# A four-layer graph attention kernel on one core: the first weighted row of a tile written into the accumulator bank by VectorE, and three instead of two dense tiles in the last layer

## The chip, the core and the metric

The kernel runs on one core of one Trainium2 chip. The metric is device time in microseconds (us) for one execution of the whole program; lower is better. Engine names: PE is TensorE (PEld its weight loads), DVE is VectorE, ACT is ScalarE, POOL is GpSimd, SP is SyncE. An "own time" is the time of the one execution that was profiled.

## What is computed

3327 nodes with 512 features pass four graph attention layers over one sparse symmetric adjacency matrix (about 16 neighbours in a row, each node its own neighbour). Each layer normalises, cuts at zero, projects, and mixes the neighbours' rows with softmax weights, one set of weights for each head:

```
h = relu(layernorm(x));  v = h @ W              # 8, 4, 1, 8 heads of 64, 128, 512, 64 columns
e[i,j] = leaky_relu(src[i] + dst[j]) where adj[i,j], else -inf
x = x + (elu of) softmax_j(e) @ v               # elu in layers 1 and 2
```

## The kernel before

**Setup.** Nodes are padded to 3328 and stand in 26 tiles of 128. The first 270 us read the adjacency matrix, list each node's neighbours, and sort the nodes by their number of neighbours. `CAPS[t]` is the longest list in sorted tile t: 36, 25, 23, 22, 21, ... down to 11, 467 in all.

**A listed tile** (`Tile`) of a layer is worked in steps of `GROUP` = 4 neighbour slots. For each slot `fetch` (gather at L834, own row by SP at L865) brings 128 rows of 528 floats from the layer's table in HBM, 2112 bytes each; slot 0 in layers 1 to 3 is the tile's own rows, a plain DMA by SP. `scored` forms z on VectorE (L887, L889) and the weights by an Exp on ScalarE (L890). `group` then multiplies each row by its weights on VectorE into the buffer `m` (L916), and TensorE adds the products up in a PSUM bank, `self.po`, by multiplying each of them with the identity (L921). A tile of K slots thus takes K VectorE products of 128x512 and K matmuls of 128x512. When the last slot is in, `divisors` (L926 to L928), `means` (L938) and `added` (L952 to L960) divide the sum and add it to `x`; in layers 0 to 2 the tile is then centred, turned (L450), cut (L457), projected (L468) and its new table row written by SP (L992). A following layer's gathers cannot start before all rows of its table are written. In the last layer `scatter` (L842) writes the tile's output rows by a POOL DMA. Layer 2 has one head; its sum is made on VectorE alone (L909, L911).

**A dense tile** is one of the tiles of highest degree that is not gathered. `DENSE = [0, 1, 9, 2]` says how many a layer has. In layers 1 and 3 the class `Several` works them: for each of 26 source tiles and each half of the heads (52 units u), SP loads half a row of the table and the mask, ScalarE forms the raw weights of 4 heads for n tiles into `r` (`weights`, L1264, 4 ACTIVATEs of 128 x 128n) and scales the features into `vs` (`features`, L1275, L1276), VectorE applies the mask (`masked`, L1280, one instruction of 128 x 512n), and TensorE multiplies (`products`, L1298, 4n matmuls with 130 columns in layer 3). `begin` (L1238, L1240) makes the targets' terms before the first unit, 2n rounds of four small matmuls and an Exp. Before a bank of such sums is used it is filled by a matmul with zeros (L1290). Layer 2's nine dense tiles have a class of their own (`Wholes`, L1150).

**Order.** POOL, PE, DVE and ACT run a written-out order. For each step s of a layer's list: gathers up to `LOOK` = 7 steps ahead, then pieces that were put down for "first" (units' masks and products, transposes), `scored` of step s+1, pieces for "scored" (the next unit's weights and features), `group` of step s, pieces for "last" (divisors, means, projections). The 52 units are spread evenly over the steps but the last 8. Gather buffers `g` are 7 deep, `m` 3 deep. Tiles go from the last (11 slots) to the first. Layer 3 has 24 listed tiles with 111 steps.

**PSUM in a layer with several heads:** pool `o` has 2 banks for the sums, `p` 1 or 2, `t` 1 or 2 (not in layer 3), `w` 1 (layer 1) or 2 (layer 3), `r` one bank for each dense tile, single-buffered.

Of the kernel before, what the change touches and what calls it, by code (L numbers as in the profile page):

```python
# [10 lines left out]
F32 = mybir.dt.float32  # L11
# [7 lines left out]
P = 128  # L19
# [6 lines left out]
BANK = 512  # L26
# [7 lines left out]
FAR = -30000.0  # L34
ROW = 528
GROUP = 4
DENSE = [0, 1, 9, 2]
ND = max(DENSE)
ROUND = 1.5 * 2.0 ** 23

# [454 lines left out]
class Slots:  # L495
# [5 lines left out]
    class Part:  # L501
        def __init__(self, pool, name, blocks):
            self.blocks, c = [], 0
            for t0, t1 in blocks:
                k = CAPS[t0] if t0 >= min(DENSE) else 1
                self.blocks.append((t0, t1, k, c))
# [17 lines left out]
def tile_gat_stack(ctx: ExitStack, tc: tile.TileContext, x, adj, adjT, ws, avs, out):  # L524
# [266 lines left out]
    with cond.Else():  # L791
        tile_gat_lists(tc, x, adj, ws, avs, out, ident, half, slots, L, low, spare, tabx, tabs)
# [3 lines left out]
def tile_gat_lists(ctx: ExitStack, tc: tile.TileContext, x, adj, ws, avs, out, ident, half, slots, L, low, spare, tabx, tabs):  # L796
# [7 lines left out]
    nc = tc.nc  # L804
# [23 lines left out]
    one, zero = [spool.tile([P, 1], F32, name=n, bufs=1) for n in ("one", "zero")]  # L828
# [10 lines left out]
    def scatter():  # L839
        while waiting:  # L840
            dst, t, rows = waiting.pop(0)
            nc.gpsimd.indirect_dma_start(out=dst, out_offset=bass.IndirectOffsetOnAxis(ap=slots(t, 0), axis=0),  # L842
                                         in_=rows, in_offset=None)

    class Tile:
# [51 lines left out]
        def group(self, i):  # L897


            H, K, wt = HEADS[self.l], CAPS[self.t], self.wt  # L900
            D = F // H
            k0, n, g = self.groups[i]
            if H == 1:
                for q in range(n):
                    v = g[:, q, :].rearrange("p (s m) -> p s m", s=2)[:, :, :F // 2]
                    acc = self.po.rearrange("p (s m) -> p s m", s=2)
                    w = wt[:, k0 + q, 0:1]
                    if k0 + q == 0:
                        nc.vector.tensor_scalar(acc, v, w, None, OP.mult)  # L909
                    else:  # L910
                        nc.vector.scalar_tensor_tensor(acc, v, w, acc, OP.mult, OP.add)  # L911
                return
            m = pools["m"].tile([P, GROUP, F], F32, name="m")
            for q in range(n):
                v = g[:, q, :].rearrange("p (s m) -> p s m", s=2)[:, :, :F // 2]
                nc.vector.tensor_tensor(m[:, q, :].rearrange("p (s h d) -> p s h d", s=2, d=D),  # L916
                                        v.rearrange("p s (h d) -> p s h d", d=D),
                                        wt[:, k0 + q, :H].rearrange("p (s h) -> p s h", s=2)
                                        .unsqueeze(3).to_broadcast([P, 2, H // 2, D]), OP.mult)
            for q in range(n):  # L920
                nc.tensor.matmul(self.po, ident, m[:, q, :], start=(k0 + q == 0), stop=(k0 + q == K - 1))  # L921

        def divisors(self):
            H, K = HEADS[self.l], CAPS[self.t]
# [424 lines left out]
    for l in range(NL):  # L1349
        W, following = following, None  # L1350
        if l == NL - 1:
            before.close()
        with ExitStack() as c2:
            def pool(name, bufs, **kw):
                return c2.enter_context(tc.tile_pool(name=f"{name}{l}", bufs=bufs, **kw))

            psum = dict(space=bass.MemoryType.PSUM)
            whole = HEADS[l] == 1
            pools = {"o": pool("ps_o", 1 if whole else 2, **psum)}
            if l < NL - 1:  # L1360
                pools.update(t=pool("ps_t", 1, **psum))
            if whole:
                pools.update(w=pool("ps_w", 3, **psum), e=pool("epool", 1))
                wholes = Wholes(l, W)
                pw = L[:, :BANK]
            else:
                pools.update(m=pool("mpool", 3))
                pools.update(p=pool("ps_p", 1 if DENSE[l] else 2, **psum))
                if DENSE[l]:
                    pools.update(w=pool("ps_w", l // 3 + 1, **psum), r=pool("ps_r", 1, **psum))  # L1370
                    if DENSE[l] > 1:
                        pools.update(e=pool("epool", 1))
                    wholes = Several(l, DENSE[l], W)
                    pw = pools["p"].tile([P, BANK], F32, name="pw")
            if DENSE[l]:

                scores = itertools.cycle([pw[:, :BANK // 2], pw[:, BANK // 2:]])
            else:
                scores = itertools.cycle([pools["p"].tile([P, BANK], F32, name="pw") for _ in range(2)])
            tiles = [Tile(l, t, W) for t in order if t >= DENSE[l]]  # L1380
            steps = [(tl, i) for tl in tiles for i in range(len(tl.k0))]
            if l == 0:
                for t in range(ND):
                    steps.insert(18 + 10 * t, (Mask(t), 0))
                steps[-8:] = [s for i, step in enumerate(steps[-8:]) for s in (step, (Ranked(i), 0))]
                steps += [(Ranked(j), 0) for j in range(8, NT)]
            if whole:
                wholes.place(len(steps) - 8)
            elif DENSE[l]:
                wholes.place(0, len(steps) - 8)  # L1390
            at_end = len(steps) + 12
            fetched = 0
            for s in range(-1, at_end):
                def do(place):
                    for piece in at.pop((s, place), []):
                        piece()
                while fetched < min(len(steps), s + LOOK):
                    steps[fetched][0].fetch()
                    fetched += 1
                do("first")  # L1400
                if s + 1 < len(steps):
                    steps[s + 1][0].scored(steps[s + 1][1])
                do("scored")
                if 0 <= s < len(steps):
                    tl, i = steps[s]
                    tl.group(i)
                    if i == len(tl.k0) - 1:
                        tl.finish(s)
                do("last")
                if s == 16 and l + 2 < NL:  # L1410
                    following = Weights(nc, wpool, work, l + 2, ws, avs)
                if l == 0 and s in (0, 1, 2):
                    for _ in range(3):
                        W.fold()
                if s >= 24 and s % 4 == 0 and following is not None:
                    following.fold()
            scatter()
            assert not at
# [42 lines left out]
```

## Time and profile before

| | |
|---|---|
| Median of 3 runs | 3030.45 us (3009.33 to 3045.77) |
| Profiled execution, own time | 2458.72 us |
| its span, first to last instruction | 2456.9 us |
| PE, DVE, POOL, ACT busy | 2082.3, 1918.9, 1751.1, 911.0 us |
| mean granted TensorE clock | 0.946 |
| gathers begin: layer 0, 1, 2, 3 | 270.9, 923.5, 1480.0, 1930.4 us |
| last gather of the last layer | 2435.1 us |

The stages follow from the gathers' own timeline: a layer's first gather waits for the last row of its table, so the pauses on POOL before 923.5, 1480.0 and 1930.4 us are the borders of the layers. Busy times are sums over an engine's instructions; a busy TensorE is not one at its peak, because matmuls overlap and their ends are modelled.

### The profile page before, as it was taken

To read this page: it belongs to the slowest core of one execution; us is meant where nothing else is said; L and a number is where in the kernel's file an instruction comes from. 1 tells how busy PE (TensorE), PEld (TensorE's weight loads), DVE (VectorE), ACT (ScalarE), POOL (GpSimd) and SP (SyncE) were. 2 spreads that over 40 slices of the span, in tenths; PEclk is the share of its full clock that TensorE was granted. 3 is DMA by queue.
4 is the path that set the end of the run, shared out by engine and by line. 5 is a ranking of instruction groups with operands and counts; after the bars stand their busy time and mean duration, and the time that the engine had idled before them with its cause. 6 is when DMAs were issued, how large, how long until landed. Compare 5 with 4: busy or idle time off the path is not lost. (4 is left out here: it accounts for less than half of the span.)

```text
span 2456.9 us, 26822 instructions
## 1 busy us (share of the span) xinstructions
PE 2082.3 (85%) x6832; PEld 1164.1 (47%) x6832; DVE 1918.9 (78%) x5004; ACT 911.0 (37%) x2506; POOL 1751.1 (71%) x1739
## 2 busy tenths in 40 slices
PE   3788689999998857989999986879696699999897
PEld 1666345455444423545455543445354455455443
DVE  6988787887767736888888865988989488787776
ACT  5877024343331113433333323443333343333330
POOL 7898467777777767776777747676666477777775
PEclk9988899999999988999999997989897899999999
DMA  6886579999988788887888857878776588888885
GB/s 229 320 297 235 173 232 290 291 291 295 278 270 237 229 230 246 263 242 235 247 260 256 253 152 254 252 243 248 217 250 186 165 250 251 242 249 248 242 242 171
DMA packets 262490, 599.55 MB, mean 244 GB/s; under 512 B 103923, under 2 KB 121331, under 8 KB 257974
## 3 DMA queue, kind: packets, MB, share of 16 engines
q0 software_dynamic: 126128, 438.08, 59.5%
q1 hardware_dynamic: 132454, 152.86, 19.3%
q10 hardware_dynamic: 3744, 6.82, 0.8%
q8 instruction: 55, 0.90, 0.1%
q14 instruction: 109, 0.89, 0.1%
HBM read 547.96 MB, written 49.65 MB: 243 GB/s over the span
## 5 line engine op out<-in xcount | busy, mean ns | idle before, releaser
L921 PE MATMUL bank<-m,ident 128*128 128x512 f32 x2608 | 1200.8, 606 | 136.3 <-DVE m L916 135.6
L916 DVE TENSOR_TENSOR m<-g,pw 128x512 f32<-128x512 f32 x1304 | 810.8, 681 | 136.9 <-ACT pw L890 130.3
L834 POOL DMA_INDIRECT g<-tab,idxb x734 | 699.7, 953 | 249.0 <-issue 166.9
L921 PEld LDWEIGHTS bank<-m,ident 128*128 128x128 f32 x2608 | 480.9, 192 | 716.3 <-issue 342.5
L468 PE MATMUL pv<-w,hT 128*128 128x264 f32 x1664 | 436.3, 417 | 66.4 <-ACT hT L457 41.3
L890 ACT ACTIVATE pw<-z 128x32 f32<-128x32 f32 (+4 forms) x362 | 69.8, 193 | 948.8 <-DVE z L889 948.7
L468 PEld LDWEIGHTS pv<-w,hT 128*128 128x128 f32 x1664 | 335.2, 205 | 168.2 <-ACT hT L457 47.5
L834 POOL DMA_INDIRECT g<-tabx,twiceb x342 | 324.2, 948 | 104.8 <-issue 77.1
L834 POOL DMA_INDIRECT g<-tab,idxa x297 | 283.3, 954 | 144.5 <-issue 79.9
L1150 PE MATMUL whole<-ve,em 128*128 128x512 f32 x468 | 230.1, 644 | 45.0 <-DVE em L1123 38.5
L694 POOL TENSOR_TENSOR key<-a,keys 128x3328 int32<-128x3328 int32 (+1 forms) x29 | 189.4, 6536 | 15.9 <-DVE cand L703 11.8
L911 DVE SCALAR_TENSOR_TENSOR bank<-g,L,bank 128x512 f32<-128x512 f32 x243 | 183.2, 754 | 6.8
L887 DVE TENSOR_TENSOR z<-g,pw 128x32 f32<-128x32 f32 (+4 forms) x362 | 63.5, 175 | 149.9 <-DMA g<-tab,idxb 48.2
L1150 PEld LDWEIGHTS whole<-ve,em 128*128 128x128 f32 x468 | 94.0, 206 | 158.2 <-issue 97.1
L834 POOL DMA_INDIRECT g<-tabx,twicea x99 | 94.6, 955 | 69.3 <-issue 32.2
L703 DVE MAX8 cand<-key 128x8 f32<-128x208 int32 x416 | 143.7, 364 | 0.1
L450 PE MATMUL pt<-ident,xn 128*128 128x128 f32 x416 | 67.6, 288 | 50.2 <-ACT hT L457 18.6
L1116 ACT ACTIVATE r<-low,mc,b 128x384 f32<-128x384 f32 x78 | 52.6, 675 | 151.3 <-DVE em L1123 127.8
L1264 ACT ACTIVATE r<-low,spare 128x256 f32<-128x256 f32 x208 | 98.9, 476 | 5.1
L889 DVE SCALAR_TENSOR_TENSOR z<-z 128x32 f32<-128x32 f32 (+5 forms) x434 | 86.1, 198 | 15.1 <-DVE z L887 0.2
L450 PEld LDWEIGHTS pt<-ident,xn 128*128 128x128 f32 x416 | 53.8, 149 | 87.7 <-issue 36.4
L431 POOL TENSOR_TENSOR rstd<-ve,half 128x1 f32<-128x1 f32 x52 | 31.9, 614 | 79.7 <-DVE ve L974 42.5
(180 smaller groups left out, 2161.9 us busy)
## 6 DMA issues: line engine op xcount, KB each, us to landing
a<-in_adj SPq DMA_DIRECT2D x25, 1664.0 KB, 8.5
tab<-v SPq DMA_DIRECT2D x78, 264.0 KB, 3.9
ve<-tab SPq DMA_DIRECT2D x78, 264.0 KB, 3.9
g<-tab SPq DMA_DIRECT2D x66, 264.0 KB, 4.2
tabx<-vx SPq DMA_DIRECT2D x26, 528.0 KB, 5.0
g<-tab,idxb POOLq DMA_INDIRECT x734, 3.9
low<-tab SPq DMA_DIRECT2D x52, 132.0 KB, 3.5
room<-tab SPq DMA_DIRECT2D x52, 132.0 KB, 3.7
```

The lines of the kernel that those rows point to most:

```text
L450: nc.tensor.transpose(pt[:, k, :], xn[:, k * P:(k + 1) * P], ident)
L468: nc.tensor.matmul(pv[:, s, :HF + 8], hT[:, k, :], W.w[:, k, s, :], start=(k == 0), stop=(k == KC - 1))
L694: nc.gpsimd.tensor_tensor(key[:, c:c + quarter], a[:, c:c + quarter], keys[:, c:c + quarter], OP.mult)
L703: nc.vector.max(cand[:, g * 8:(g + 1) * 8], key[:, g * SEG:(g + 1) * SEG])
L834: nc.gpsimd.indirect_dma_start(out=out_, out_offset=None, in_=table, in_offset=bass.IndirectOffsetOnAxis(ap=which, axis=0))
L889: nc.vector.scalar_tensor_tensor(z, z, SLOPE, z, OP.mult, OP.max)
L890: nc.scalar.activation(self.wt[:, k0:k0 + n, :H], z, AF.Exp)
L911: nc.vector.scalar_tensor_tensor(acc, v, w, acc, OP.mult, OP.add)
L916: nc.vector.tensor_tensor(m[:, q, :].rearrange("p (s h d) -> p s h d", s=2, d=D), v.rearrange("p s (h d) -> p s h d", d=D), wt[:, k0 + q, ...
L921: nc.tensor.matmul(self.po, ident, m[:, q, :], start=(k0 + q == 0), stop=(k0 + q == K - 1))
L1150: nc.tensor.matmul(tl.po.rearrange("p (s m) -> p s m", s=2), e[:, q * P:(q + 1) * P], v.rearrange("p (s m) -> p s m", s=2)[:, :, :F // 2], ...
L1264: nc.scalar.activation(self.r[:, h, :], self.a[:, g, :], AF.Relu, bias=-1.0, scale=self.b[:, j, g:g + 1])
```

## The change

Three things are altered. In layers with several heads, the product of slot 0 is written by VectorE to the tile's PSUM bank instead of `m`, and the identity matmul of slot 0 is left out; the remaining matmuls of the tile add to what stands in the bank (`start=False`). At the start of each of these layers both banks of pool `o` are written once by a matmul with zeros. And the last layer has three dense tiles instead of two: tile 2, with 23 slots, is no longer gathered, and `r` takes three banks.

```diff
-DENSE = [0, 1, 9, 2]
+DENSE = [0, 1, 9, 3]
...
             for q in range(n):
                 v = g[:, q, :].rearrange("p (s m) -> p s m", s=2)[:, :, :F // 2]
-                nc.vector.tensor_tensor(m[:, q, :].rearrange("p (s h d) -> p s h d", s=2, d=D),
+
+                out_ = self.po if k0 + q == 0 else m[:, q, :]
+                nc.vector.tensor_tensor(out_.rearrange("p (s h d) -> p s h d", s=2, d=D),
                                         v.rearrange("p s (h d) -> p s h d", d=D),
                                         wt[:, k0 + q, :H].rearrange("p (s h) -> p s h", s=2)
                                         .unsqueeze(3).to_broadcast([P, 2, H // 2, D]), OP.mult)
-            for q in range(n):
-                nc.tensor.matmul(self.po, ident, m[:, q, :], start=(k0 + q == 0), stop=(k0 + q == K - 1))
+            for q in range(k0 == 0, n):
+                nc.tensor.matmul(self.po, ident, m[:, q, :], start=False, stop=(k0 + q == K - 1),
+                                 skip_group_check=True)
...
+            if not whole:
+
+                for _ in range(2):
+                    nc.tensor.matmul(pools["o"].tile([P, BANK], F32, name="bank"), ident,
+                                     zero.to_broadcast([P, BANK]), start=True, stop=True)
```

## The prediction

> **What bounds the kernel now.** I began with the page: span, busy times, costliest groups.
>
> ```profile
> PE 2082.3 (85%) x6832; PEld 1164.1 (47%) x6832; DVE 1918.9 (78%) x5004; ACT 911.0 (37%) x2506; POOL 1751.1 (71%) x1739
> L921 PE MATMUL bank<-m,ident 128*128 128x512 f32 x2608 | 1200.8, 606 | 136.3 <-DVE m L916 135.6
> L916 DVE TENSOR_TENSOR m<-g,pw 128x512 f32<-128x512 f32 x1304 | 810.8, 681 | 136.9 <-ACT pw L890 130.3
> ```
>
> By the sums TensorE looks like the bound, and identity matmuls are over half of it. But the shares average four layers, so next came the busy times in stretches (columns: PE, PEld, DVE, ACT, POOL busy with counts, clock, DMA share, GB/s), one stretch from each of layers 0, 1 and 3.
>
> ```profile
> 297.00:840.00 543.00, 493.38 (x1553) 254.76 (x1554) 421.89 (x1120) 168.03 (x436) 402.60 (x425) 0.98 0.87 268
> 1040.00:1400.00 360.00, 347.05 (x1094) 189.65 (x1093) 309.40 (x822) 137.94 (x423) 261.60 (x276) 1.00 0.84 248
> 1950.00:2436.00 486.00, 448.58 (x1622) 241.32 (x1620) 384.42 (x803) 169.44 (x599) 368.05 (x388) 0.99 0.82 244
> ```
>
> POOL shows only 74 to 76%, the lowest of the three. Its timeline explains that:
>
> ```profile
> 2251.83 0.95 POOL L834 DMA_INDIRECT g<-tab,idxb  x1 [0.30 <-issue]
> 2253.08 0.95 POOL L834 DMA_INDIRECT g<-tab,idxb  x1 [0.30 <-issue]
> 2254.34 0.95 POOL L834 DMA_INDIRECT g<-tab,idxb  x1 [0.30 <-issue]
> ```
>
> Each gather starts 1.25 us after the one before and waits for nothing but "issue". This pitch holds almost without a break from 331 to 910 us and from 1930.4 us to the end: POOL is full there, at a displayed 76%. Layer 3 has 382 gathers and 26 output DMAs on POOL: 382 x 1.2525 + 26 x 1.29 = 512 us, against the 511 from its first gather (1930.4) to where its stream breaks (2441.2). Its waits and its part of the chain agree (us in total, times, longest; then shares):
>
> ```profile
> PE bank L921 <- DVE m L916: 48.7, 39, 10.4
> DVE z L887 <- DMA g<-tab,idxb: 47.5, 41, 2.4
> DVE m L916 <- ACT pw L890: 36.5, 103, 2.8
> POOL g L834 <- DVE m L916: 12.5, 41, 0.3
> ```
>
> VectorE waits for gathers to land, TensorE waits for VectorE, and POOL's wait for a buffer is never over the usual 0.3 us gap. In layer 1 the stream breaks between 1072 and 1222 us, some 16 us beyond the pitch in all. There VectorE is the late one: TensorE waited 12.5 us for L916 and VectorE nothing for L921. So in this execution layers 0 and 3 are bound by POOL, layer 1 by VectorE and POOL; nowhere between the borders does TensorE set the pace.
>
> **What the skill says.** The Trainium skill, "Perfetto Trace Analysis", section "DMA Instruction — SWDGE (GPSIMD)": the profiled end of such a DMA is the end of descriptor generation, not of the data's movement. The trace agrees: 0.95 us on POOL, 3.9 us to landing. "PSUM — Partial Sum Buffer", section "The four PSUM rules": VectorE writes neither set nor clear the written bits, and a matmul without the first flag adds where the bit is set. That is why each bank needs one matmul over its full width before VectorE seeds it, so the change can do what it says; no run here shows this yet. "VectorE: DVE Perf Modes", section "The TRN2 errata": an fp32 tensor_tensor takes (N+151)/0.96 ns, 691 for 512; the trace has 681. It has no price for a PSUM destination; the trace does.
>
> **The change part by part.** Unit prices, from the timelines of layer 3:
>
> ```profile
> 1964.29 1.95 PE L1298 MATMUL whole<-spare,low 128*128 128x130 f32 x16
> 1966.08 7.03 PE L921 MATMUL bank<-m,ident 128*128 128x512 f32 x16
> 1967.23 2.48 DVE L916 TENSOR_TENSOR m<-g,pw 128x512 f32<-128x512 f32 x4 [0.33 <-ACT pw L890]
> ```
>
> An fp32 matmul is two instructions. L921 starts 1.79 us after L1298: eight products, 0.224 us each. The row after L921 starts at 1972.94: eight identity matmuls in 6.86, 0.858 each. Four products on VectorE take 2.48, one alone 0.68, so each further one is 0.60.
>
> 1. Slot 0 to the bank. It takes 26, 25 and 23 identity matmuls from layers 0, 1 and 3: 22.3, 21.5 and 19.7 us of TensorE. The VectorE instruction stays and changes its destination. Instructions that write `bank` take 691 to 694 ns (L938, L952), the tensor_scalar of L909 746; so 74 instructions cost 1 to 5 us of VectorE, none below nothing, since the element count is the same. I take 0: outside 1072 to 1222 us its waits for gathers cover it. No new wait stands in VectorE's order: the bank's last reader is `added` two tiles earlier, before this write on VectorE itself. In layers 0 and 3 the removed matmuls lie beside a full POOL: 0. In layer 1 they help only where TensorE is late, at the end:
>
> ```profile
> 1463.42 1.02 PE L921 MATMUL bank<-m,ident 128*128 128x512 f32 x2
> 1464.48 0.70 DVE L938 TENSOR_TENSOR bank<-bank,den 128x512 f32<-128x512 f32 x1 [6.92 <-PE bank L921]
> ```
>
> VectorE waits 6.92 us, and TensorE had run without a pause since 1428.6, in which only tile 1's slot 0 lies. One matmul: -0.9 us. At layer 0's end TensorE waits for VectorE: 0.
>
> 2. Six zero matmuls, 5.2 us of TensorE at three starts. TensorE there waits 10 us for the first product in layers 1 and 3: 0.
>
> 3. The third dense tile, all in layer 3.
> POOL: tile 2 has 23 slots, one by SP, so 22 gathers go: 22 x 1.2525 = -27.6 us; the 26 output DMAs stay. SP loses one own-row DMA; its 52 mask loads grow from 32 to 48 KB.
> TensorE: 23 identity matmuls more go (-19.7, with part 1 -39.5); 52 units get 4 products more, 208 x 0.224 = +46.6. Net +7.1.
> VectorE: the mask grows from 1024 columns (1.21 us) to 1536; with 256 at 0.413 the slope is 1.04 ns, so 1.74: 52 x 0.53 = +27.7. Gone are 23 products (13.8), six steps' z, their wait for Exp (about 4.3) and a tile's divisors and mean (1.4); net about +9 with the longer dense means.
> ScalarE: 208 ACTIVATEs grow from 476 ns to 585 (slope from 128 columns, 367) or 675 (L1116, 384 columns): +23 to +42, on an engine busy 169 of 486 us: hidden.
> Start: `begin` gets two more rounds of 1.85 us; with the zeros its last Exp would end near 1939.4 instead of 1933.6, 1 us past the first Exp of z (1938.33) queued behind it. Seven buffers cover it: 0, at worst 1.
>
> What is late next? Up to 2410 us, where the units end, TensorE needs 413 of 467 us before. After, 420 of 439: 19 us left, 4%. VectorE's 47.5 us of waiting for gathers lose 27.6 and 9: 11 left. Both still fit, but narrowly: masks come in lumps of 1.74 us, `m` is three deep, `r` single. I charge 5 us, between 0 and 20.
>
> Sum: -27.6 + 5 - 0.9 = -23.5, so the profiled execution goes from 2458.7 to 2435.2, a ratio of 0.9904. The median of the runs is 1.2325 times the profiled execution; nothing in the trace says by what. I carry the ratio over: 3030.45 x 0.9904 = 3001. Were the extra 572 us fixed, it would be 3007; were it all a slower gather, 22 x 1.54 = 34 us, 2996.
>
> **Rivals.**
> B, TensorE sets the pace in the timed runs (a lower clock would stretch them). For it: 85% busy, 96% in layer 1. Against: its waits for L916. Then -22.3 - 21.5 + 7.1 = -36.7, times 1.2325: 2985; with layer 3 still bound by POOL, 2947.
> C, layer 3's gain is swallowed: VectorE or TensorE takes over where POOL lets go. For it: the 11 and 19 us above. Against: gather buffers seven deep. Only the 0.9 remains: 3029.
> D, slower: TensorE's waits for VectorE stay in layer 3 and each unit's longer mask lengthens one. TensorE needs 441 there and waits 48.7, together 490, hidden under POOL's 511. After: 449 + 48.7 + 27.7 = 525, 14 to 16 over 511: with 16, 2475 us, carried over 3050. It decides once waits exceed 483 - 449 = 34 us. Against: with POOL ahead, VectorE finds its gathers landed and its own waits shrink.
> That the bank is not seeded (bits clear) would alter values, not time.
>
> **How the numbers follow.** Forecast 0.48, B 0.12, C 0.20, D 0.20. About 1% is what a measurement of this kernel can tell from no change. The forecast's own range is 2985 to 3015, so nearly half of it is faster by over 1%; with B that makes 0.36. C, the rest of the forecast and a third of D are within 1%: 0.47. D with a longer wait: 0.17. The range reaches from B's lower end to past D: 2950 to 3060.
>
> **What would show it.** Right: 1009 gathers of g by index instead of 1031 (734 + 297) outside layer 0; layer 3's stream near 483 us at the 1.25 pitch; L921 with 2414 instructions; L1298 with 1456; layers 0 and 1 as long as before within 2 us. Wrong: gathers in layer 3 that wait for L916 for over 0.3 us; VectorE waiting for L921 or L1298; ScalarE's features waiting for L1298; layers 0 or 1 shorter by over 5 us.

## The result, and the profile after

The kernel after takes 2979.34 us (median of 4 runs, 2973.41 to 2982.78), the kernel before on the same chip 3019.89 us. The ratio is 0.9854, with a 95% interval of 0.9819 to 0.9889: faster, by about 1.5%. The forecast ratio was 0.9904, on 3030.45 us 3001, a gain of 29 us; 40.6 were measured.

Chips differ here: one execution of either kernel takes about 3000 us on the chip of this result and about 2460 us on the chips of most experiments, so a ratio is always between runs on one chip, and times are read from traces only where both stand near 2460 us. The profiled execution of before shown above, 2458.72 us beside runs of 3030, evidently came from a chip of the second kind.

The page of the kernel after (3000 us chip), the rows that answer to those shown of before:

```profile
PE 2211.9 (74%) x7082; PEld 1246.1 (42%) x7082; DVE 1923.1 (65%) x4968; ACT 934.6 (31%) x2502; POOL 1731.4 (58%) x1717
L923 PE MATMUL bank<-m,ident 128*128 128x512 f32 x2414 | 1232.2, 659 | 335.9 <-DVE m L918 197.3
L918 DVE TENSOR_TENSOR m<-g,pw 128x512 f32<-128x512 f32 x1207 | 752.5, 682 | 384.1 <-ACT pw L890 209.2
L918 DVE TENSOR_TENSOR bank<-g,pw 128x512 f32<-128x512 f32 x74 | 51.5, 696 | 100.7 <-ACT pw L890 69.2
```

From this page counts and unit prices can be read. The identity matmul has 2414 instructions, as predicted. The product is split: 1207 go to `m`, 74 to the bank. A write to the bank costs 14 ns more, 1 us over all 74. Lines have moved by up to three: L916 is now L918, L921 is L923, L1264 is L1267, L1280 is L1283, L1298 is L1301.

One thing more has to be read on this chip, because the forecast was about it: layer 3 of the kernel after does not look as predicted here. The longest of POOL's waits for another engine between 2400 and 2900 us (us in total, times, longest), and the chain of the layer by line (shares of the stretch from 2313 us on):

```profile
POOL g L834 <- DVE m L918: 91.7, 21, 8.2
```

```profile
by line: PE bank L923 28.3%; issue 25.5%; PE whole L1301 13.2%; another core or an unknown queue 9.7%; DVE m L918 8.8%; ACT r L1267 3.7%; ACT L L1278 2.3%; DVE room L1283 2.0%; ACT pw L890 0.8%; DVE z L889 0.7%; DVE z L887 0.7%; POOL g L834
```

POOL waits for VectorE's products, up to 8.2 us at a time, and has a share of under 1% of the chain; TensorE has over 40%. So what follows shows the cause on the chips near 2460 us; that it is the cause of the measured gain on this chip is not shown.

For the times, both kernels were run on one chip near 2460 us (`e1_before` and `e4_both` below). The busy times in stretches (columns: stretch and length, then PE, PEld, DVE, ACT and POOL busy with counts, clock, DMA share, GB/s), first the kernel before, then the kernel after. The stretches are layer 0, layer 1, and layer 3 up to its last gather:

```profile
297.00:840.00 543.00, 489.50 (x1543) 253.65 (x1544) 418.99 (x1114) 168.49 (x436) 401.62 (x425) 0.98 0.87 268
1040.00:1400.00 360.00, 348.25 (x1086) 189.88 (x1086) 309.39 (x823) 136.73 (x418) 261.23 (x277) 0.99 0.84 249
1952.00:2438.00 486.00, 447.97 (x1623) 240.81 (x1621) 385.02 (x805) 169.57 (x599) 368.09 (x388) 0.99 0.83 245
```

```profile
297.00:840.00 543.00, 479.95 (x1498) 247.50 (x1498) 417.36 (x1113) 168.25 (x436) 401.92 (x425) 0.97 0.87 268
1040.00:1400.00 360.00, 338.59 (x1063) 184.97 (x1061) 311.35 (x830) 137.23 (x422) 261.23 (x277) 0.99 0.84 249
1952.00:2409.00 457.00, 447.06 (x1947) 272.44 (x1946) 393.77 (x769) 189.31 (x599) 345.81 (x366) 0.99 0.83 247
```

In layers 0 and 1 TensorE loses about 10 us in each stretch, but POOL issues the same 425 and 277 DMAs in the same time: nothing is won there. In layer 3 the kernel after gets from 1952 to its last gather 29 us sooner, with 22 POOL DMAs fewer.

The layers, each from its first gather to the next layer's, the last to the end of the span (times from POOL's timeline), and layer 3 in its two parts, from the first gather to the last and from there to the end:

| us | layer 0 | layer 1 | layer 2 | layer 3 | its gathers | behind them |
|---|---|---|---|---|---|---|
| before (`e1_before`) | 653.4 | 555.9 | 450.1 | 525.6 | 504.1 | 21.5 |
| after (`e4_both`) | 652.0 | 554.4 | 450.7 | 496.0 | 475.3 | 20.7 |

In neither of the two streams of gathers in layer 3 does POOL idle for more than 0.32 us at once. Layer 3 gives 29.6 of the 30.2 us by which the span is shorter (2458.5 to 2428.3). The waits in layer 3's stretch, first before, then after (engine, who waits for whom: us in total, times, longest):

```profile
DVE z L887 <- DMA g<-tab,idxb: 45.7, 41, 3.2
DVE m L916 <- ACT pw L890: 38.4, 103, 2.9
PE bank L921 <- DVE m L916: 37.4, 38, 2.4
```

```profile
DVE m L918 <- ACT pw L890: 39.1, 77, 4.0
DVE bank L918 <- ACT pw L890: 11.9, 22, 1.9
PE bank L923 <- DVE m L918: 9.8, 10, 3.2
ACT L L1278 <- PE whole L1301: 6.7, 5, 3.3
```

VectorE no longer waits for gathers in this stretch: the 45.7 us are gone from the list. TensorE waits 9.8 us for VectorE instead of 37.4. So POOL is still full, but the others stand close behind it, and the layer has hardly any slack left on any of the three: of 457 us TensorE is busy 447; VectorE is busy 394 and waits 51 for Exp, 445 together; POOL's 366 DMAs at a gap of 0.30 us take 346 + 110 = 456.

### The profile page after: what moved, and what is told of

Its sections match the earlier page's. It is cut to its first block, busy times and chain, and to the rows that moved or that the text cites. A ratio compares the mean times of both kernels' runs of the same rounds, so it can differ in the third digit from the quotient of the medians.

```text
span 2971.7 us, 27155 instructions
## 1 busy us (share of the span) xinstructions
PE 2211.9 (74%) x7082; PEld 1246.1 (42%) x7082; DVE 1923.1 (65%) x4968; ACT 934.6 (31%) x2502; POOL 1731.4 (58%) x1717
## 4 chain that ended last, share of the span: by engine, by line
PE 24%; DVE 18%; issue 14%; another core or an unknown queue 8%; ACT 5%; POOL 3%; DMA 2%; SPq 0%; DVEq 0%; POOLq 0%; ACTq 0%
PE bank L923 16%; DVE m L918 6%; PE pv L468 4%; PE whole L1301 3%; DVE bank L911 3%; POOL g L834 3%; ACT r L1267 1%; DVE z L889 1%; DVE z L887 1%; DVE x L961 1%; PE whole L1153 1%; DMA g<-tab,idxb 1%; DVE em L1126 1%; DVE q L438 1%
## 5 line engine op out<-in xcount | busy, mean ns | idle before, releaser
L923 PE MATMUL bank<-m,ident 128*128 128x512 f32 x2414 | 1232.2, 659 | 335.9 <-DVE m L918 197.3
L918 DVE TENSOR_TENSOR m<-g,pw 128x512 f32<-128x512 f32 x1207 | 752.5, 682 | 384.1 <-ACT pw L890 209.2
L834 POOL DMA_INDIRECT g<-tab,idxb x712 | 678.8, 953 | 482.0 <-issue 197.1
L923 PEld LDWEIGHTS bank<-m,ident 128*128 128x128 f32 x2414 | 488.8, 211 | 942.1 <-issue 582.4
L1301 PE MATMUL whole<-L,room 128*128 128x130 f32 x1248 | 173.3, 290 | 59.9 <-issue 59.5
L1301 PEld LDWEIGHTS whole<-L,room 128*128 128x128 f32 x1248 | 164.7, 202 | 91.4 <-issue 89.7
L475 ACT ACTIVATE v<-pv,rstd 128x528 f32<-128x528 f32 x78 | 54.2, 694 | 274.4 <-remote 126.5
L1267 ACT ACTIVATE r<-low,L 128x384 f32<-128x384 f32 x208 | 121.2, 583 | 16.9 <-remote 9.5
L918 DVE TENSOR_TENSOR bank<-g,pw 128x512 f32<-128x512 f32 x74 | 51.5, 696 | 100.7 <-ACT pw L890 69.2
```

Of the source, the lines that this page charges most:

```text
L834: nc.gpsimd.indirect_dma_start(out=out_, out_offset=None, in_=table, in_offset=bass.IndirectOffsetOnAxis(ap=which, axis=0))
L918: nc.vector.tensor_tensor(out_.rearrange("p (s h d) -> p s h d", s=2, d=D), v.rearrange("p s (h d) -> p s h d", d=D), wt[:, k0 + q, :H].re ...
L923: nc.tensor.matmul(self.po, ident, m[:, q, :], start=False, stop=(k0 + q == K - 1), skip_group_check=True)
L1267: nc.scalar.activation(self.r[:, h, :], self.a[:, g, :], AF.Relu, bias=-1.0, scale=self.b[:, j, g:g + 1])
L1301: nc.tensor.matmul(dst, e[:, h, q * P:(q + 1) * P], mov, start=False, stop=(j == NT - 1), skip_group_check=True)
```

## The experiments

All but two ran on two chips near 2460 us. "Layer 3" is measured as in the table, in one trace of each kernel. Kernels whose layer 3 is the same agree in it within 1 us: 525.6 and 526.5 for the kernel before, 495.9 to 496.0 for three that have both parts there.

**The two parts apart.** The kernel before again; the seeding alone; the third dense tile alone; both.

```diff
 e2_seed_only: the kernel after with
-DENSE = [0, 1, 9, 3]
+DENSE = [0, 1, 9, 2]
 e3_dense_only: the kernel before with
-DENSE = [0, 1, 9, 2]
+DENSE = [0, 1, 9, 3]
```

> The kernel before, unchanged, to have its trace beside the change's (2971.7 us of span, of which layers 0, 1, 2 and 3 take 843, 737, 459 and 658 us by the first gathers at 273.7, 1117.3, 1854.6 and 2313.6 us). The trace seen ahead of the prediction had 653, 557, 450 and 527. Theory T (gathers, as predicted): the new trace of before is as long as the runs, near 3020, layers 0 to 2 equal the change's within 10 us, and layer 3 alone is longer, by about 35 us. Rival S (slot 0): layers 0 and 1 are longer than the change's by 20 us or more in sum, layer 3 about the same.

> Slot 0 written to the bank and the zero matmuls, but two dense tiles in the last layer as before. Theory T (the gain is the shorter stream of gathers in layer 3): same as before, ratio 0.997 to 1.003. Rival S (the gain is the 74 matmuls taken from TensorE, which sets the pace in the timed runs): ratio about 0.985. Half and half: 0.992.

> Three dense tiles in the last layer, slot 0 by TensorE as before. Theory T: ratio 0.987 to 0.99, the whole gain, all of it in layer 3. Rival S: the 23 identity matmuls of tile 2 (19.7 us) go and 208 products (46.6 us) come, so TensorE has 27 us more in layer 3: ratio 1.005 or more. Half and half: 0.993.

> The change itself once more, on the chip of the two halves: ratio 0.982 to 0.989. If the halves add, it is the product of the ratios of the two kernels with one half each; if the third dense tile only pays once slot 0 has made room on TensorE, the product is nearer to 1 than this.

| kernel | median us | ratio to before (95%) | layer 3 |
|---|---|---|---|
| `e1_before` | 2460.1 | 0.9999 (0.999 to 1.0008) | 525.6 |
| `e2_seed_only` | 2461.24 | 1.0007 (0.9998 to 1.0017) | 526.1 |
| `e3_dense_only` | 2432.94 | 0.9886 (0.987 to 0.9903) | 500.7 |
| `e4_both` | 2430.07 | 0.9869 (0.9853 to 0.9886) | 496.0 |

The first was expected near 3020 us, to be laid beside the trace of the result; it ran on a chip near 2460 us, so that comparison could not be made. The seeding alone takes 75 identity matmuls (layer 3 has 24 listed tiles then), 64 us by the 0.858 us of the prediction, off TensorE and is worth nothing. The dense tile alone brings nearly all. Layer 3's stretch of the dense tile alone, its waits (us in total, times, longest), and its chain by line (shares of the stretch):

```profile
1951.00:2408.00 457.00, 454.80 (x1981) 277.63 (x1980) 387.36 (x758) 187.24 (x593) 346.03 (x365) 1.00 0.84 247
```

```profile
DVE m L916 <- ACT pw L890: 56.7, 95, 3.7
ACT L L1275 <- PE whole L1298: 13.4, 6, 3.8
PE bank L921 <- DVE m L916: 2.1, 2, 1.4
```

```profile
by line: PE bank L921 46.4%; PE whole L1298 21.4%; DMA g<-tab,idxa 5.7%; issue 5.1%; DVE m L916 5.0%; POOL g L834 4.4%; ACT r L1264 2.4%; DVE room L1280 2.3%; ACT L L1275 1.6%; DMA g<-tab,idxb 1.5%; DMA out<-x,idxa 0.8%; PE whole L1290 0.8%
```

Without the seeding TensorE is full: 454.8 of 457 us, and two thirds of the chain. The waits suggest that its lateness reaches VectorE by way of ScalarE: the features wait 13.4 us for products (L1298) to be done with their buffers, the Exp behind them in ScalarE's order comes late, and VectorE waits 56.7 us for Exp instead of 38.4 (with both parts 6.7 and 51.0). No gather waits for it: from the first gather to the last there are 475.3 us here too, as with both parts. The lateness comes out behind the last gather, where 25.4 us pass to the end instead of 20.7. With the seeding the chain of the same stretch is shared again, as this line of `e4_both` shows, against that of the kernel before below it:

```profile
by line: PE bank L923 23.4%; DVE m L918 12.2%; PE whole L1301 11.0%; DMA g<-tab,idxb 10.6%; issue 10.1%; ACT r L1267 6.9%; POOL g L834 6.4%; DVE room L1283 4.6%; ACT L L1278 2.8%; DMA g<-tab,idxa 2.4%; ACT pw L890 1.5%; DVE z L889 1.4%; DVE
```

```profile
by line: DMA g<-tab,idxb 28.8%; POOL g L834 18.8%; issue 16.4%; DVE m L916 14.9%; PE bank L921 2.6%; DMA g<-tab,idxa 2.4%; ACT r L1264 1.8%; DVE z L889 1.7%; ACT pw L890 1.6%; DVE low L1280 1.6%; DVE z L887 1.5%; ACT spare L1275 1.2%; DMA o
```

The chain goes from gathers and POOL (the kernel before) to TensorE (dense tile alone) to a mixture (both). In layer 3 the seeding is then worth 4.7 us, all of it behind the last gather, and in the medians 2.9; the two ratios' intervals overlap, so its size is known only to a few us. The product of the two halves' ratios is 0.9893, against 0.9869 with both: the parts help each other a little, by no more than the intervals are wide.

**Seeding in the last layer only.** The kernel after, with slot 0 going to `m` and its matmul kept in layers 0 and 1 (there with `start` again, and without the zero matmuls; these two edits are not shown).

```diff
-                out_ = self.po if k0 + q == 0 else m[:, q, :]
+                out_ = self.po if self.l == NL - 1 and k0 + q == 0 else m[:, q, :]
...
-            for q in range(k0 == 0, n):
+            for q in range(k0 == 0 and self.l == NL - 1, n):
```

> The change with slot 0 written to the bank in the last layer alone; layers 0 and 1 as before. If the 3 us by which the whole change beats the kernel with the third dense tile alone come from layer 3, where TensorE was full: ratio 0.986 to 0.988, like the whole change. If they come from layers 0 and 1: 0.988 to 0.990, like the third dense tile alone.

Measured: 2428.97 us, 0.9865 (0.9845 to 0.9886), layer 3 495.9 us. The whole gain is there: the seeding in layers 0 and 1 adds nothing that can be measured.

**POOL relieved without the dense tile.** In layer 3 the last slot of each listed tile is read by a plain SP DMA of 128 rows instead of a gather: 24 gathers fewer in the kernel before, 23 in the kernel after. The rows are the tile's own, as many bytes as before but not the neighbours', so these kernels do not compute the layer's output; they are for the time alone.

```diff
+                elif l == NL - 1 and k0 + q == CAPS[t] - 1:
+                    nc.sync.dma_start(g[:, q, :], tabs[l % 2][t * P:(t + 1) * P, :])
                 elif l > 0:
```

> The kernel before, but in the last layer the last slot of each of the 24 listed tiles is brought by a plain DMA of SP (the tile's own rows, same bytes) instead of a gather: POOL loses 24 gathers there, no other engine loses or gains an instruction but SP. The output is no longer the reference's. Theory T (a gather costs its 1.2525 us of POOL's stream): -30.1 us, less what the tile-to-tile slack of 11 us on VectorE and some 50 us on TensorE does not cover, so -24 to -30, ratio 0.988 to 0.990. Rival (the bytes or landings bound the stream, not POOL's issue): 0 to -5 us, ratio 0.998 to 1.000.

> The changed kernel with the same replacement in the last layer (23 listed tiles, 23 gathers fewer on POOL, 28.8 us of its stream; the output is no longer the reference's). If POOL still sets the pace there by a wide margin: -25 to -29 us against the change. If TensorE, busy 447 of 457 us in that stretch, is next: -10 us at most, ratio to before 0.983 to 0.987.

> The changed kernel with 23 gathers of the last layer brought by SP (output not the reference's) once more, as the partner of the next run on the same chip. It took 494.9 us in layer 3 against the change's 496.0, with POOL's waits up from 7 to 22 us: so layer 3 should be no shorter than the change's again.

Before with it: 2426.91 us against 2460.61, 0.986 (0.9839 to 0.988). That is 33.7 us, more than expected; layer 3 shortens by 31.2 (525.6 to 494.4), of which 24 gathers at 1.2525 explain 30.1. No other engine but SP gained or lost an instruction, so this alone shows that POOL set the pace of layer 3. The kernel after with it: 2427.09 us, 0.9869 (0.9847 to 0.9891), and again 2426.37 us, 0.9867 (0.9847 to 0.9887). Here 23 gathers fewer, 28.8 us of POOL, shorten layer 3 by only 1.1 to 1.3 us (to 494.9 and 494.7), and POOL now waits for others. The waits of POOL in `e11_sp_rows_both_2`, layer 3:

```profile
POOL g L834 <- DVE m L920: 13.0, 20, 2.2
POOL g L834 <- DVE pw L887: 8.9, 7, 4.4
```

The longest are 2.2 and 4.4 us, where with POOL as the slowest none was over its own 0.3 us gap. The stream of gathers, which had no break, now loses 17.4 us to waits, so it is shorter by 11.4 us instead of 28.8; and behind the last gather 30.8 us pass instead of 20.7. The third dense tile thus closed the distance between POOL and the engines behind it almost to the last microsecond.

**What stands right behind POOL: TensorE or VectorE?** The kernel of `e11_sp_rows_both_2`, and in layer 3 the identity matmul of slot 1 left out too (each tile's sum lacks that row besides). First on the chip near 3000 us, then on the other.

```diff
-            for q in range(k0 == 0, n):
+            for q in range((2 if self.l == NL - 1 else 1) if k0 == 0 else 0, n):
```

> The changed kernel with 23 gathers of the last layer brought by SP, and besides in that layer the matmul of slot 1 left out (23 matmuls, 19.7 us of TensorE; VectorE still forms the products; the output is no longer the reference's). If TensorE is what bounds the last layer once POOL has let go: 10 to 20 us less than the kernel with the SP rows alone. If VectorE is (394 of 457 us busy, and its waits for the Exp): 0 to 5 us less.

> The same, and in the last layer the matmul of slot 1 left out as well (23 matmuls, 19.7 us of TensorE; VectorE still forms the products). Run before where all executions took a fifth longer, with 0.9863 (0.980 to 0.9925), too wide to tell. If TensorE bounds layer 3 once POOL has let go: 10 to 20 us less than its partner, layer 3 near 480 us. If VectorE does, with its waits for the Exp: 0 to 5 us less, layer 3 at 490 or more.

The first was inconclusive: 2942.45 us against 2981.12, 0.9863 with an interval of 0.98 to 0.9925. The second: 2425.21 us, 0.9861 (0.9845 to 0.9877), layer 3 490.3 us instead of 494.7. The medians lie only 1.2 us apart, which is not told apart; the layer's length is what can be read. Its stretch of layer 3 below that of `e11_sp_rows_both_2`:

```profile
1952.00:2400.00 448.00, 437.95 (x1931) 268.55 (x1930) 385.30 (x754) 188.23 (x594) 326.12 (x344) 0.99 0.84 252
```

```profile
1952.00:2400.00 448.00, 425.76 (x1890) 261.04 (x1890) 389.05 (x760) 192.03 (x606) 327.20 (x345) 0.99 0.84 254
```

and the waits of the second in the same stretch:

```profile
DVE m L920 <- ACT pw L892: 37.5, 77, 3.4
DVE bank L920 <- ACT pw L892: 12.6, 23, 1.9
PE bank L925 <- DVE m L920: 26.7, 22, 7.6
```

TensorE lost 23 matmuls, 19.7 us; the layer 4.4. TensorE's wait for VectorE rose from 10.0 to 26.7 us, while VectorE is busy or waiting for Exp for 389 + 50 = 439 of 448 us. The likeliest reading is that VectorE with its waits for Exp stands within about 5 us behind TensorE; a run that relieves VectorE, which would show it, was not made.

**Layer 1's late pieces.** In layer 1 the next layer's preparations are put into the order from step 64 on instead of 24, to take VectorE's work out of the part where its gathers' stream breaks.

```diff
-                if s >= 24 and s % 4 == 0 and following is not None:
+                if s >= (64 if l == 1 else 24) and s % 4 == 0 and following is not None:
```

> The change, and in layer 1 the folding of the last layer's weights (8 pairs L408 and L410, 1.37 us of VectorE each, at steps 24 to 52) put off to steps 64 to 92. The prediction read the breaks of layer 1's stream of gathers (15 us in all) as VectorE being late in its small tiles. If so: 5 to 11 us less than the change, ratio 0.982 to 0.985, and the breaks under 8 us. If the breaks have another cause, or the folds are as late in the larger tiles: 0.986 to 0.988.

Measured: 2427.61 us, 0.9858 (0.9837 to 0.988): not told apart from `e4_both`. The mechanism came, the gain did not: layer 1's breaks (what its stream of gathers loses to the 1.25 us pitch) shrink from 15.4 to 9.1 us, but the layer lasts 554.3 us against 554.4. The first gather of layer 2 in POOL's timeline, in `e4_both` and then here (start, us, what, idle before it and its releaser):

```profile
1481.64 0.94 POOL L834 DMA_INDIRECT g<-tab,idxa  x1 [31.69 <-DMA tab<-v]
```

```profile
1485.23 0.94 POOL L834 DMA_INDIRECT g<-tab,idxa  x1 [37.76 <-DMA tab<-v]
```

POOL waits 6 us longer for the table's last row: once the gathers come sooner, layer 1's end is set by the chain to that row and not by them.

**TensorE loaded where it is said to be idle.** The kernel before with a second matmul, of zeros, for each tile's slot 0 in layers 0, 1 and 3: 75 of 0.858 us, 64 us.

```diff
+                if k0 + q == 0:
+                    nc.tensor.matmul(self.po, ident, zero.to_broadcast([P, BANK]), start=False, stop=False,
+                                     skip_group_check=True)
```

> The kernel before with one more matmul per listed tile in layers 0, 1 and 3 (identity times zeros into the tile's sum, 75 in all, 64 us of TensorE), the mirror of the removed ones. Theory T (TensorE does not set the pace before the change): ratio 0.999 to 1.003, of that about +1 us at the end of layer 1. Rival S (it does in layers 0 and 1): +40 us or more, ratio 1.016.

Measured on the chip near 3000 us: 3001.13 us against 2981.12, 1.0072 (1.0048 to 1.0096). Neither expectation holds: 20 us are not nothing, and not the 40 us or more that were expected of a TensorE that sets the pace in layers 0 and 1. Whether the same load would be free on a chip near 2460 us was not tried.

## Why the prediction was right, point by point

What follows is measured on the chips near 2460 us. There the mechanism is the forecast's, gathers taken from a full POOL. On the chip of the result the change gained as large a share (0.9854, against 0.9869), but POOL was not full in layer 3 of that trace, and no run there takes the change apart. That a share worked out on a trace of 2459 us held at 3000 us is therefore partly luck: the factor 1.2325 was that between two chips, and not something in the program.

**Slot 0 to the bank, 0.** Right as far as layers 0 and 1 go, and for the seeding alone (1.0007). The -0.9 us at layer 1's end has its trace: VectorE's wait for the last bank, in `e4_both`,

```profile
1465.86 0.70 DVE L941 TENSOR_TENSOR bank<-bank,den 128x512 f32<-128x512 f32 x1 [5.66 <-PE bank L923]
```

against 6.92 us before: -1.3. It is the same 6.92 in `e3_dense_only` and `e7_seed_last_only`, which do not seed layer 1 (and in `e8_fold_late`, which does, but in another order of pieces). In the layer's length it cannot be told from the spread between traces. In layer 3 it was wrong to price the seeding and the dense tile as a sum of separate terms. Once the third tile fills TensorE, the 19.7 us that the seeding takes away in this layer are no longer all beside a full POOL.

**The third dense tile, -27.6.** Right. Counts agree: 712 + 297 = 1009 gathers of g outside layer 0, and L1301 1248 + 208 = 1456 instructions. Layer 3's 475.3 us from first to last gather are 28.9 fewer than before: 22 x 1.2525 = 27.6, and one output DMA more that falls behind the last gather (1.3). The part behind them, shorter by 0.8, makes the 29.6 whole. With all output DMAs but the last, which waits for its tile, the stream ends after 482.6 us, by the prediction 483. (The prediction's 512 us for the stream before count all 26 output DMAs; 25 lie ahead of the break at 2441.2 us, which makes 510.7, closer still to the 511.) This also agrees with what the Trainium skill says under "Perfetto Trace Analysis", section "DMA Instruction — SWDGE (GPSIMD)", that the displayed end is the end of descriptor generation and not of the data's movement: a removed gather showed 0.95 us and gave back its pitch on POOL, 1.25, not the 3.9 us to its landing.

**The unit prices.** VectorE's mask, predicted 1.74 us, and ScalarE's weights, put between 585 ns by the slope and 675 by the nearest row, in layer 3 of `e4_both`:

```profile
L1283 DVE SCALAR_TENSOR_TENSOR room<-r,L 128x1536 f32<-128x1536 f32 x17 | 29.7, 1746 | 0.1
L1267 ACT ACTIVATE r<-low,L 128x384 f32<-128x384 f32 x200 | 116.5, 583 | 4.9
```

VectorE's net +9 looks met, 393.8 - 385.0 = +8.8, but is not the same sum: the prediction had taken off 4.3 us of waits for Exp, and these did not fall but rose by 12.6, from 38.4 to 51.0. So the 11 us that VectorE was to have left were gone. TensorE's +7.1 did not show: its displayed busy time went from 448.0 to 447.1, the products' +46.4 against -46.0 for the identity matmuls, where 39.5 were predicted. The displayed time of identity matmuls is above their pitch of 0.858 us in both traces (0.917 us a product before, 0.907 after, as estimated from busy time over counts), so it is no clean measure of the work.

**The give-back, +5: the term that was mis-sized.** It measured about 0 with both parts; with the dense tile alone it was 2.7 us, as 27.6 less the 24.9 by which layer 3 is shorter. Even there the stream of gathers gave nothing back; the cost arose behind the last gather. I put the cost on the change, with VectorE's slack of 11 us and TensorE's 19; both shrank to almost nothing, yet POOL's gap was not exceeded. That the seven gather buffers took up the lateness is likely, but no run varied them. So -23.5 was short of the -29.9 of the medians (2459.96 to 2430.07) by 5 of give-back and, for most of the rest, 1.3 of the output DMA. The carried ratio was 0.9904, measured 0.9869 on the one chip and 0.9854 on the other.

**The signs of being wrong.** Of the four named, gathers that wait over 0.3 us for the product and layers 0 or 1 shorter by over 5 us did not appear in `e4_both`. VectorE waiting for TensorE stayed small (3.7 us in layer 3's stretch, 2.4 before). Features waiting for products did appear, 6.7 us, without reaching the gathers. On the chip of the result the first sign did appear, with waits of up to 8.2 us. It was to speak against the forecast, and there it does.

**The rivals.** C, the gain swallowed, and D, slower, fell: D wanted TensorE's waits for VectorE to stay, and in layer 3's stretch they fell from 37.4 to 9.8 us once VectorE found its gathers landed. B, TensorE sets the pace, fell on the chips near 2460 us: seeding without the dense tile brought nothing, and relieving POOL alone brought all. On the chip near 3000 us it stays open. For it: B's 2985 us is a ratio of 0.985, and there 0.9854 was measured, with 0.9904 outside the interval; and TensorE has over 40% of the chain of layer 3 there. Against it: 64 us more of TensorE cost only 20 there, and the same change gives a ratio within 0.002 of this where B is refuted. The seeding alone was not run there. The chances were also added up wrongly: C with the other half of the forecast and a third of D make 0.51 for "within 1%", not 0.47, and leave 0.13 for a longer time, not 0.17.

## What to carry to other kernels

Read an engine's load as its work plus the gap between its instructions: POOL at a displayed 76% was full, and TensorE at 92% was not the bound. A saving is worth nothing beside a full engine, but when another part of the change relieves that engine, price the parts together: the seeding was worth 0 alone and about 3 us with the third dense tile. Look also behind the end of a stream: with the dense tile alone TensorE was full, yet no gather waited, and the 4.7 us were paid after the last one. And before relieving an engine further, see how far behind the next one is: here 23 more gathers taken from POOL bought one microsecond.

## What the runs showed of the hardware

A VectorE product of 128x512 fp32 costs hardly more with PSUM as its destination: 696 ns against 682. I had bounded it by 5 us in all and it was 1. A bank that a matmul had once written over its full width could be seeded by VectorE with values other than zero, 74 times in one execution: the matmuls without `start` added to them, and the output of the kernel after is the right one. Beyond that, the same program, the kernel before, takes 2460 us on one chip and 2981 on another, with a mean granted clock of 0.946 in its profiled executions on the one and of 0.867 to 0.880 in its runs on the other. A clock lower by a factor of 1.08 does not make up a time longer by 1.21; what does was not settled. The pitch of the gathers where nothing holds them, 1.25 us, is the same on both.
